# The 7x7 convolution of a two-block kernel: banded weight rows loaded to half of the partitions, and copied by VectorE to the other half

## The chip, the cores and the metric

The kernel runs on one core of one Trainium2 chip. Its metric is the device time of one execution in microseconds (us). Three runs of the kernel before took 6082.45, 6082.88 and 6088.8 us; the median is 6082.88.

The engines have short names in the profile: PE is TensorE (matrix products), PEld its weight loads, DVE is VectorE, ACT is ScalarE, POOL is GpSimd and SP is SyncE. SP, ScalarE and GpSimd can issue DMAs; GpSimd's have the DMA queue q0, and SP's have q1.

## The reference

The input x has 8 images of 96 x 96 pixels with 192 channels in fp32. The first block normalises x by groups, projects it to 384 channels, applies a depthwise 3x3 convolution and four running averages, normalises over channels, projects back and adds x. The second block is the one that matters here:

```python
def _L1_conv_ref(x, dw_kernel, dw_bias, ln_gamma, ln_beta, w0, b0, w1, b1, gamma):
    y = lax.conv_general_dilated(x, dw_kernel, window_strides=(1, 1), padding='SAME',
            dimension_numbers=('NHWC', 'HWIO', 'NHWC'), feature_group_count=c) + dw_bias
    ...
    y = (y - mu) * lax.rsqrt(var + EPS) * ln_gamma + ln_beta
    y = jnp.einsum('bhwc,cd->bhwd', y, w0) + b0
    y = jax.nn.gelu(y, approximate=False)
    y = jnp.einsum('bhwd,dc->bhwc', y, w1) + b1
    return y * gamma

x = x + _L1_conv_ref(_gn(x), ...)
```

`_gn` is the normalisation over 32 groups of 6 channels of each image. The convolution is depthwise: each channel has its own 7 x 7 filter (the weights are `dw_kernel`, 7 x 7 x 1 x 192).

## The kernel before

The work runs in five stages, each with its own pools of tiles, and each ends before the next one's products begin: the first projection (to about 847 us of the span), the 3x3 convolution with the running averages (to 1885), the second projection of the first block (to 3003), the 7x7 convolution (to 3590) and the two dense layers of the second block (to the end). In each stage the order of instructions on every engine is the order of the program (`tc.manual_schedule()`); nothing is reordered by a planner.

**The 7x7 convolution as products.** Its input lies in DRAM as `X1_d`, by rows and by three column phases; 21 image rows times 3 phases make 63 lines, which lie on 63 of 64 partitions. A product of TensorE contracts over these 63 lines with a band matrix, which holds the filter's taps along a diagonal band, so that one product gives the outputs of 63 lines for one horizontal offset. The bands of all channels were prepared in DRAM as `Z2_d` (64 rows, 192 channels, `ZW` = 208 numbers). The stage uses the two halves of the partitions at the same time: the lower half (0 to 63) works on row blocks 0, 2 and 4, the upper half (64 to 127) on row blocks 1, 3 and 5. Both halves contract with the same band, and since a product reads its weights from the partitions that its data are on, the band has to be in both halves.

**Loads.** The 192 channels make 32 groups m of `HC` = 6 channels. `load_d(m)` loads what one group needs: a tile `xin`, in three pieces t for each half (384 KB each, line 748), and a tile `band`, one load for each half (64 partitions of 6 x 208 numbers, 4992 bytes each, 312 KB, line 753). What goes to the lower half is issued by SP, what goes to the upper half by GpSimd. So each of the two queues carries three pieces of xin and one band for each group. Five groups can be held at a time (`ND` = 5: one buffer that is there early, and four more in the pool `d_in`); a load waits for its buffer's last reader on TensorE.

**Scaling.** `scale_d(m, xin)` applies the group normalisation to xin in place, with one VectorE instruction for each of the 8 images (line 1006).

**Products and stores.** `conv_d` makes the products of one channel for a pair of groups (line 1021), which ScalarE brings from PSUM into the tile `yo` with the bias (line 1032). `store_d` writes `yo` to DRAM as `Y_d`, with 16 DMAs from GpSimd a turn (line 1061); the last turn divides them between SP and GpSimd (line 1060). A turn of the loop handles a pair of groups, and there are 16 turns. Turn i first issues the loads of groups 2i+3 and 2i+4, then the scaling of groups 2i+2 and 2i+3 for the next turn, then the products of groups 2i and 2i+1, and then its stores:

```python
for i in range(n_i):
    pair, loads = loads[:2], loads[2:]
    for m in (2 * i + 3, 2 * i + 4):
        if m < 2 * n_i:
            loads.append(load_d(m))
    if i + 1 < n_i:
        for k in range(2):
            scale_d(2 * i + 2 + k, loads[k][1])
```

On GpSimd's queue a turn is therefore eight loads, which are the three pieces and the band of the odd group and then those of the even group, and after them sixteen stores. A DMA of this queue waits until the DMA eight places ahead of it has landed, because eight semaphores are used in turn. SP's queue has the same eight loads, and no stores except in the last turn. VectorE has only the scalings in this stage.

The functions that the change touches, with the lines of the profile:

Of the kernel before, what the change touches and what calls it, by code (L numbers as in the profile page):

```python
# [84 lines left out]
def conv_blocks_kernel(  # L85
# [31 lines left out]
    nc = tc.nc  # L117
# [44 lines left out]
    Z2_d = dram.tile([64, D, ZW], F32, name="Z2_d")  # L162
# [126 lines left out]
    with ExitStack() as ph:  # L289
# [175 lines left out]
        with tc.manual_schedule():  # L465
# [9 lines left out]
            for b in range(B):  # L475
                more = b + 1 < B
                for t in range(n_t):
# [27 lines left out]
                    k, j = divmod(t, NJ)  # L505
# [32 lines left out]
    with ExitStack() as ph:  # L538
# [13 lines left out]
        def load_b(k):  # L552
            c = slice(k * CC, (k + 1) * CC)
            band = bp_.tile([128, CC, 3, RB], F32, tag="band", name=f"band0_{k}")
            pin = bp_.tile([128, CC, GB, NJ, S], F32, tag="pin", name=f"pin_{k}")
            for g in range(NG):
                p = g * 64
                nc.sync.dma_start(
                    band[p : p + RB + 4].rearrange("p c t o -> p (c t o)"),
                    ZB_d[:, c].rearrange("r c t o -> r (c t o)"),  # L560
                )
                for lo, hi in ((0, RB), (RB, RB + 1), (RB + 1, RB + 2)):
                    nc.sync.dma_start(
                        pin[p + lo : p + hi].rearrange("p c b j h -> p c (b j h)"),
                        P_d[g, c, lo:hi].rearrange("c r b j h -> r c (b j h)"),
                    )
            return band, pin
# [71 lines left out]
        with tc.manual_schedule():  # L639
            loads = [load_b(k) for k in range(3)]  # L640
# [8 lines left out]
            for n in range(NI * (n_k + 1)):  # L649
                k, i = divmod(n, NI)  # L650
                z = None
                if k < n_k:
                    if i == 0:
                        band, pin = loads.pop(0)
# [48 lines left out]
    def make_weights(ps):  # L703
        for m in range(NE):
            for p, k, _ in spans[:2]:
                nc.tensor.matmul(
                    ps[:, m : m + 1],
                    w0w[p, k, m * 128 : (m + 1) * 128],
                    aff[p, k, 1:2],
                    start=(k == 0),  # L710
                    stop=(k == 1),
                )
        nc.vector.tensor_tensor(b1g, b1g, lsc, ALU.mult)
        for m in range(NE):
            nc.vector.tensor_tensor(w1g[:, m], w1g[:, m], lsc, ALU.mult)
        nc.vector.tensor_tensor(b0g, b0g, ps[:, :NE], ALU.add)
        for k in range(3):
            nc.vector.tensor_scalar(w0w[:, k], w0w[:, k], aff[:, k, 0:1], None, ALU.mult)
# [9 lines left out]
    HC = GS  # L728
# [6 lines left out]
    def load_d(m):  # L735
        c = m * HC
        row = D * WV * 2
        pool = d_pools[m % ND > 0]
        xin = pool.tile([128, NT, BP, HC, 2 * WV], F32, tag="xin", name="xin")

        for t in range(NT):
            for g, eng in enumerate((nc.sync, nc.gpsimd)):
                src = bass.AP(
                    tensor=X1_d.tensor,
                    offset=X1_d.offset + (2 * t + g) * HG * PH * row + c * WV * 2,
                    ap=[[row, 64], [S * PH * row, BP], [1, HC * WV * 2]],
                )
                eng.dma_start(
                    xin[g * 64 : (g + 1) * 64, t].rearrange("q a c n -> q a (c n)"), src
                )  # L750
        band = pool.tile([128, HC, ZW], F32, tag="band", name="band1")
        for g, eng in enumerate((nc.sync, nc.gpsimd)):
            eng.dma_start(
                band[g * 64 : (g + 1) * 64].rearrange("q c l -> q (c l)"),
                Z2_d[:, c : c + HC].rearrange("r c l -> r (c l)"),
            )
        return band, xin

    s1 = s1_pool.enter_context(tc.tile_pool(name="s1", bufs=1)).tile(
# [2 lines left out]
    with ExitStack() as ph:  # L762
# [175 lines left out]
        with tc.manual_schedule():  # L938
            load_weights()
            for u in range(n_u + 1):  # L940
# [22 lines left out]
                if held is not None:  # L963
                    k, t = divmod(u - 1, n_c)
# [8 lines left out]

            stores.pop(0)()
            first_d = load_d(0)
            for store in stores:
                store()
# [10 lines left out]
    with ExitStack() as ph:  # L988
# [9 lines left out]
                dw_bias.rearrange("(i k c) -> k i c", k=2, c=HC)[k].partition_broadcast(64),  # L998
            )

        def scale_d(m, xin):
            xv = xin.rearrange("q t a c (v b) -> q t a c v b", b=2)
            for b in range(B):
                sc, sh = (s1[:, a, b % 2, b // 2, m : m + 1] for a in range(2))
                xw = xv[:, :, b // 2, :, :, b % 2]
                nc.vector.tensor_scalar(xw, xw, sc, sh, ALU.mult, ALU.add)  # L1006
# [33 lines left out]
        def store_d(yo, i):  # L1040
            for bl in range(NB):

                pieces = [(3, HB - 3)]
                if bl == 0:
                    pieces.append((HB - 3, HB))
                if bl == NB - 1:
                    pieces.append((0, 3))
                for k in range(2):
                    c = i * CD + k * HC
                    for lo, hi in pieces:  # L1050
                        r = (S - HB - bl * HG) * PH
                        src = yo[k * 64 + lo * PH : k * 64 + hi * PH, bl]
                        dst = Y_d[r + lo * PH : r + hi * PH, :, :, c : c + HC].rearrange(
                            "r b a c n -> r (b a) (c n)"
                        )
                        src = src.rearrange("r a c n -> r a (c n)")

                        n = NV if i == D // CD - 1 else 0
                        if n:
                            nc.sync.dma_start(dst[:, :n], src[:, :n])  # L1060
                        nc.gpsimd.dma_start(dst[:, n:], src[:, n:])

        n_i = D // CD
        with tc.manual_schedule():
            loads = [first_d] + [load_d(m) for m in range(1, 3)]
            make_weights(ps_y.tile([128, 512], F32, tag="py1", name="ps_b0"))
            for m in range(2):
                scale_d(m, loads[m][1])
            for i in range(n_i):
                pair, loads = loads[:2], loads[2:]  # L1070
                for m in (2 * i + 3, 2 * i + 4):
                    if m < 2 * n_i:
                        loads.append(load_d(m))
                if i + 1 < n_i:
                    for k in range(2):
                        scale_d(2 * i + 2 + k, loads[k][1])
                yo = op.tile([128, NB, BP * NV, HC, 2 * WQ], F32, tag="yo", name=f"yo_{i}")
                for c in range(HC):
                    conv_d(pair, c, yo, i)
                store_d(yo, i)  # L1080
# [233 lines left out]
```

## Time and profile before

| What | Value |
|---|---|
| median of 3 runs | 6082.88 us |
| the profiled execution's own time | 6083.09 us |
| its span, from the first to the last instruction | 6081.0 us |
| 7x7 stage, 3003 to 3590 us | 587 us |
| PE busy in that stage | 414.21 us |
| DVE busy in that stage | 167.40 us |
| POOL busy in that stage | 245.80 us |
| products of line 1021 | 6912 |
| scalings of line 1006 | 256, median 665 ns |
| loads of band, line 753 | 32 from SP and 32 from GpSimd |
| HBM read, written | 585.19 MB, 476.57 MB |

The profile comes from one execution. It records for every instruction its engine, line, operation, start and duration, and what ended the idle time before it. A line of a view in order of time begins with the start and the duration in us; "x432" says that so many instructions are merged into it, and "[7.95 <-DVE xin L1006]" that the engine had been idle for 7.95 us until VectorE's instruction of line 1006, which writes xin, had ended. In rows of 40 slices, each digit is the busy share of a slice in tenths. "DMA share" is the mean busy share of the 16 DMA engines, and PEclk the granted clock of TensorE as a share of full speed. A DMA that GpSimd issues shows as a POOL instruction, whose duration is that of the issue; the transfer itself comes later.

### The profile page before, as it was taken

What the parts mean: (1) busy time and instruction counts of PE and PEld (TensorE: products, weight loads), DVE (VectorE), ACT (ScalarE), POOL (GpSimd) and SP (SyncE); (2) the same over time, 40 slices, a digit from 0 to 9 for tenths busy, and PEclk for the clock granted to TensorE, in tenths of its full rate; (3) what the DMA queues carried; (4) which work ended last, traced back from release to release, by engine and by line L of the source; (5) the groups of instructions that cost most, each with busy time, mean ns of one, the idle gap of its engine ahead of it and who ended that gap; (6) DMA issues with size and microseconds to landing.
All of it is one profiled execution on the core that took longest, in us unless ns stands there. A gap on an engine that the chain in (4) does not pass through costs nothing.

```text
span 6081.0 us, 122820 instructions
## 1 busy us (share of the span) xinstructions
PE 5685.5 (93%) x48550; PEld 3948.3 (65%) x48550; DVE 3456.3 (57%) x8026; ACT 2438.4 (40%) x6146; POOL 2632.8 (43%) x2832
## 2 busy tenths in 40 slices
PE   4899989999998999999777759999999999999999
PEld 2455543333335989898666647777777777777777
DVE  5455539999996667777632334444444444444442
ACT  2344447777775555555433322222222222222221
POOL 0111128888886666666544433222222222322222
PEclk9899989999999999999888879999999999999999
DMA  8987669999997888888799962222222222222221
GB/s 238 230 246 238 210 191 244 245 245 242 244 244 203 253 261 267 262 265 263 230 287 286 291 167 78 63 78 62 78 62 77 63 78 63 78 63 78 63 63 37
DMA packets 570206, 1054.36 MB, mean 173 GB/s; under 512 B 109575, under 2 KB 426260, under 8 KB 567328
## 3 DMA queue, kind: packets, MB, share of 16 engines
q1 hardware_dynamic: 385312, 577.65, 35.9%
q0 software_dynamic: 124160, 450.67, 23.9%
q10 hardware_dynamic: 60160, 18.20, 1.5%
q8 instruction: 384, 6.29, 0.5%
q14 instruction: 190, 1.56, 0.1%
HBM read 585.19 MB, written 476.57 MB: 175 GB/s over the span
## 4 chain that ended last, share of the span: by engine, by line
PE 75%; DMA 7%; DVE 1%; issue 1%; POOL 1%; SPq 1%; ACT 0%; POOLq 0%; DVEq 0%; ACTq 0%
PE po L1213 19%; PE po L830 13%; PE hp L1183 12%; PE pl L576 10%; PE hp L1193 7%; PE pa L597 4%; PE pt L828 4%; DMA xin<-X_d 4%; PE pt L1166 2%; PE pa L600 2%; DMA Y_d<-yo 2%; PE py L1021 1%; DMA band<-Z_d 1%; DVE xin L1006 0%; SPq L1060 0%
## 5 line engine op out<-in xcount | busy, mean ns | idle before, releaser
L1202 ACT ACTIVATE g<-hp,b0g 128x384 f32<-128x384 f32 x1152 | 573.9, 580 | 1856.3 <-PE hp L1193 1856.3
L1213 PE MATMUL po<-w1g,g 128*128 128x192 f32 x6912 | 1178.3, 327 | 0.0
L1213 PEld LDWEIGHTS po<-w1g,g 128*128 128x128 f32 x6912 | 1116.6, 190 | 1.6 <-issue 1.1
L830 PE MATMUL po<-wc,mt 128*96 128x193 f32 x4608 | 913.3, 334 | 0.0
L1170 DVE COPY yT<-pt 128x384 f32<-128x384 f32 x288 | 251.4, 873 | 1126.9 <-PE pt L1166 1126.6
L1231 POOL DMA_DIRECT2D out_dram<-xo x576 | 321.2, 560 | 1148.0 <-DVE xo L1220 1119.5
L1183 PE MATMUL hp<-yT,w0w 128*128 128x384 f32 x2304 | 794.5, 488 | 0.4 <-ACT g L1202 0.4
L830 PEld LDWEIGHTS po<-wc,mt 128*96 128x96 f32 x4608 | 702.3, 163 | 68.4 <-ACT mean L834 65.0
L576 PE MATMUL pl<-pin,band 34*32 34x380 f32 (+1 forms) x13824 | 628.6, 489 | 18.5 <-DMA pin<-P_d 18.5
L1183 PEld LDWEIGHTS hp<-yT,w0w 128*128 128x128 f32 x2304 | 431.5, 191 | 231.5 <-issue 2.8
L606 DVE TENSOR_TENSOR_SCAN z<-decay,loc 128x768 f32<-128x768 f32 x288 | 505.8, 1756 | 59.1 <-ACT loc L585 29.3
L1021 PE MATMUL py<-xin,band 63*64 63x248 f32 (+1 forms) x6912 | 405.9, 393 | 141.6 <-DVE xin L1006 139.6
L646 POOL TENSOR_TENSOR mo<-mo,z 128x768 f32<-128x768 f32 x288 | 529.4, 1839 | 3.4 <-ACT mo L601 0.4
L615 DVE TENSOR_TENSOR_SCAN z<-decay,z 128x768 f32<-128x768 f32 x288 | 498.1, 1730 | 0.0
L576 PEld LDWEIGHTS pl<-pin,band 34*32 34x32 f32 x13824 | 233.1, 107 | 396.1 <-issue 394.8
L1021 PEld LDWEIGHTS py<-xin,band 63*64 63x64 f32 x6912 | 343.4, 142 | 203.7 <-DVE xin L1006 125.6
L837 ACT ACTIVATE sq<-pt,mean 96x384 f32<-96x384 f32 x768 | 442.9, 577 | 25.9 <-ACT mean L834 1.0
L1193 PE MATMUL hp<-yT,w0w 64*128 64x384 f32 x2304 | 449.5, 508 | 0.0
L597 PE MATMUL pa<-loc,mix 128*32 128x384 f32 x3456 | 431.9, 493 | 0.0
L600 PE MATMUL pa<-last,down 96*32 96x384 f32 x1152 | 426.8, 493 | 0.9 <-ACT mo L601 0.9
L29 POOL TENSOR_TENSOR rs<-rs_ve,neg_half 96x8 f32<-96x8 f32 x96 | 158.6, 1652 | 607.1 <-DVE rs_ve L28 607.1
L375 PE MATMUL pm<-xT,win 128*128 128x384 f32 x1152 | 401.5, 500 | 20.0 <-ACT xT L368 19.7
(116 smaller groups left out, 7712.8 us busy)
## 6 DMA issues: line engine op xcount, KB each, us to landing
P_d<-po POOLq DMA_DIRECT2D x96, 1152.0 KB, 8.8
pin<-P_d SPq DMA_DIRECT2D x192, 576.0 KB
mt<-M_d SPq DMA_DIRECT2D x576, 192.0 KB
xq<-in_x_dram SPq DMA_DIRECT2D x96, 576.0 KB
xr<-in_x_dram SPq DMA_DIRECT2D x384, 144.0 KB
X_d<-x1u POOLq DMA_DIRECT2D x192, 288.0 KB, 4.1
X_d<-x1c SPq DMA_DIRECT2D x192, 288.0 KB
y<-Y_d SPq DMA_DIRECT2D x24, 2304.0 KB
```

The source lines that it names most:

```text
L576: nc.tensor.matmul(pls[g][at * RB : (at + 1) * RB, :, lo:hi], band[rows, c, kh, :], pin[rows, c, :, NJ - 1 - j, lo + kh - 1 : hi + kh - 1] ...
L597: nc.tensor.matmul(pa[at], mix[:, i, at], loc[:, q], start=True, stop=True)
L600: nc.tensor.matmul(pa[at], down[:, to], last[:, q], start=True, stop=True)
L606: nc.vector.tensor_tensor_scan(zf, decay_f, loc.rearrange("p q n -> p (q n)"), 0.0, ALU.mult, ALU.add)
L615: nc.vector.tensor_tensor_scan(zr, decay_f, zr, 0.0, ALU.mult, ALU.add)
L646: nc.gpsimd.tensor_tensor(m, m, z, ALU.add)
L830: nc.tensor.matmul(po[:S, b], lhs[m], wc[:, m], start=(m == 0), stop=(m == NC - 1))
L1021: nc.tensor.matmul(pys[t // 2][g][k * 64 : (k + 1) * 64, t % 2, :, lo:hi], pair[k][0][rows, c, d * ZS : d * ZS + 64], pair[k][1][rows, t, ...
L1183: nc.tensor.matmul(hps[m, q], w0w[:, 2 * q, m * 128 : (m + 1) * 128], yT[:, 2 * q], start=True, stop=False,)
L1193: nc.tensor.matmul(hps[m, q], w0w[p, 1, m * 128 : (m + 1) * 128], yT[p, 1], start=False, stop=True,)
L1202: nc.scalar.activation(g[:, m, q], hps[m, q], AF.Gelu, bias=b0g[:, m : m + 1], scale=1.0)
L1213: nc.tensor.matmul(po[:, q], g[:, m, q, k * 128 : (k + 1) * 128], w1g[:, m], start=(m == 0), stop=(m == NE - 1),)
```

## The change

`load_d` issues one load of the band in place of two. For an even group it is SP's, into the lower half of the partitions, and for an odd group GpSimd's, into the upper half. `scale_d` is given the band as well, and begins with a VectorE copy of the loaded half to the other one, ahead of the eight scalings of the group.

```diff
         band = pool.tile([128, HC, ZW], F32, tag="band", name="band1")
-        for g, eng in enumerate((nc.sync, nc.gpsimd)):
-            eng.dma_start(
-                band[g * 64 : (g + 1) * 64].rearrange("q c l -> q (c l)"),
-                Z2_d[:, c : c + HC].rearrange("r c l -> r (c l)"),
-            )
+
+        g = m % 2
+        (nc.sync, nc.gpsimd)[g].dma_start(
+            band[g * 64 : (g + 1) * 64].rearrange("q c l -> q (c l)"),
+            Z2_d[:, c : c + HC].rearrange("r c l -> r (c l)"),
+        )
         return band, xin
...
-        def scale_d(m, xin):
+        def scale_d(m, band, xin):
+            g = m % 2
+            nc.vector.tensor_copy(
+                band[(1 - g) * 64 : (2 - g) * 64], band[g * 64 : (g + 1) * 64]
+            )
             xv = xin.rearrange("q t a c (v b) -> q t a c v b", b=2)
             for b in range(B):
...
             for m in range(2):
-                scale_d(m, loads[m][1])
+                scale_d(m, *loads[m])
...
                     for k in range(2):
-                        scale_d(2 * i + 2 + k, loads[k][1])
+                        scale_d(2 * i + 2 + k, *loads[k])
```

The products of line 1021 wait for VectorE's copy where they waited for a DMA of the band; their number, order and operands stay as they were.

## The prediction

> **What bounds the kernel now.** I read the page first, then the busy time by stage, then the 7x7 stage alone: PE and VectorE in order of time, the DMA traffic of two of its turns, and GpSimd's queue in order of time. The page:
>
> ```profile
> span 6081.0 us, 122820 instructions
> PE   4899989999998999999777759999999999999999
> DMA  8987669999997888888799962222222222222221
> ```
>
> Only the dip of PE near slice 20 is touched. The profiled execution took 6083.09 us, 2.1 us more than its span; the median of the runs shown is 6082.88, so its own sum can stand for it. Busy time of each engine in the 7x7 stage and in the one behind it:
>
> ```profile
> core 0: us, PE busy (x) PEld busy (x) DVE busy (x) ACT busy (x) POOL busy (x), PEclk, DMA share, GB/s
> 3003.00:3590.00 587.00, 414.21 (x6944) 350.95 (x6944) 167.40 (x303) 201.50 (x384) 245.80 (x385) 0.83 0.99 269
> 3590.00:6081.00 2491.00, 2449.93 (x12672) 1828.41 (x12672) 1124.06 (x2976) 575.22 (x1153) 729.10 (x768) 0.99 0.25 69
> ```
>
> In its 587 us PE works 414 and the DMA engines all the time. Three of the sixteen turns on PE, and the scalings of xin on DVE around them (start, duration, and in brackets the idle time before and what ended it):
>
> ```profile
> 3214.14 25.68 PE L1021 MATMUL py<-xin,band 63*64 63x256 f32 x432 [7.95 <-DVE xin L1006]
> 3248.66 25.49 PE L1021 MATMUL py<-xin,band 63*64 63x256 f32 x432 [8.84 <-DVE xin L1006]
> 3280.78 25.28 PE L1021 MATMUL py<-xin,band 63*64 63x256 f32 x432 [6.63 <-DVE xin L1006]
> ```
> ```profile
> 3243.87 4.74 DVE L1006 TENSOR_SCALAR xin<-xin,s 128x576 f32<-128x576 f32 x8 [20.99 <-DMA xin<-X_d]
> 3250.69 4.80 DVE L1006 TENSOR_SCALAR xin<-xin,s 128x576 f32<-128x576 f32 x8 [2.09 <-DMA xin<-X_d]
> 3275.98 4.74 DVE L1006 TENSOR_SCALAR xin<-xin,s 128x576 f32<-128x576 f32 x8 [20.49 <-DMA xin<-X_d]
> ```
>
> PE idles 7 to 9 us a turn, for DVE, which has itself been idle 20 us for xin. From the turn that starts at 3082.15 to the last at 3546.67 there are 14 periods: 33.18 us each. The scaling at 3243.87 is that of the odd group (m = 2i+3), which PE needs at once; that at 3250.69 is the even one for the turn after. Traffic from 3214 to 3282, in 40 slots of 1.7 us:
>
> ```profile
> GB/s 305 373 328 340 297 342 325 384 393 394 386 328 202 209 206 200 204 205 195 289 340 362 316 308 348 398 382 388 369 342 305 231 212 200 209 208 199 201 235 301
> q0 software_dynamic: 4128, 13.57, 73.2%
> q1 hardware_dynamic: 3780, 6.29, 30.7%
> ```
>
> q0 is GpSimd's queue, q1 SP's (packets, MB, share of the 16 engines' time). SP moves less than half as much and spends its time waiting for PE to free a buffer (258.5 us for xin, line 748, between 3083 and 3572). So GpSimd's queue is the long one: 8 loads and 16 stores a turn. How it runs:
>
> ```profile
> 3237.12 0.54 POOL L753 DMA_DIRECT2D band<-Z_d x1 [0.52 <-DMA Y_d<-yo]
> 3239.51 0.70 POOL L1061 DMA_DIRECT2D Y_d<-yo x1 [1.85 <-ACT yo L1032]
> 3240.52 0.58 POOL L1061 DMA_DIRECT2D Y_d<-yo x1 [0.30 <-DMA xin<-X_d]
> 3243.76 0.80 POOL L1061 DMA_DIRECT2D Y_d<-yo x1 [2.66 <-DMA xin<-X_d]
> 3245.07 0.56 POOL L1061 DMA_DIRECT2D Y_d<-yo x1 [0.51 <-DMA band<-Z_d]
> 3247.32 0.73 POOL L1061 DMA_DIRECT2D Y_d<-yo x1 [1.68 <-DMA xin<-X_d]
> 3248.83 0.63 POOL L1061 DMA_DIRECT2D Y_d<-yo x1 [0.78 <-DMA xin<-X_d]
> 3250.59 0.81 POOL L1061 DMA_DIRECT2D Y_d<-yo x1 [1.13 <-DMA xin<-X_d]
> 3252.03 0.62 POOL L1061 DMA_DIRECT2D Y_d<-yo x1 [0.64 <-DMA band<-Z_d]
> ```
>
> Each store waits for the DMA eight places ahead to land, so these starts are the landings of the loads, one behind another without a gap: xin third piece at 3243.76, band at 3245.07, then the even group's pieces and its band at 3252.03. The stores are issued while up to 12 us of loads are still ahead of them. A period is this queue's work: by the landings about 16 us of loads and 17 of stores. The flat slots near 203 GB/s are its loads alone.
>
> **The change part by part.** Each group's band is now one load of 64 x 4992 bytes = 0.32 MB in place of two: even groups on SP into the lower half, odd ones on GpSimd into the upper. A turn fetches one odd and one even group, so each queue loses one band of two a turn.
>
> (1) GpSimd's queue, on the path. A band there cost 1.31 us (3243.76 to 3245.07) and 1.44 (3250.59 to 3252.03); its bytes at 203 GB/s are 1.57. I take 1.45; ends 1.3 and 1.6. The even bands of m = 4 to 30 fall in the 14 periods.
>
> (2) SP's queue, beside it. That band only shares the 16 DMA engines with GpSimd's stores. From below it is 0: between 3572 and 3610, after all loads of the stage, its last stores and the next stage's first load move 201 GB/s, so stores don't take up all that is left to them. From above: both bands at the mean rate of these two turns (294 GB/s) are 0.64/0.294 = 2.17 us, less 1.45 leaves 0.7. I take 0.3, nearer to the row of stores alone. The queue alone would then need 33.18 - 1.45 - 0.3 = 31.4.
>
> (3) The copies, 32 of 64 x 1248 on DVE. Bounds by element: the contiguous scaling of w0w (line 718, 768 in 615 ns) gives 1.00 us, the strided copy of x1c (line 866, 768 in 1050 ns) 1.71. I take 1.0, since operands here are contiguous too. The even one has cover: its group lands a turn ahead; if that cover went, it would cost 1.0 a turn. The odd one has none.
>
> (4) A new wait. scale_d now starts with the copy, and the copy waits for the band, behind the three xin pieces on its queue. Queued behind it on DVE are the eight scalings of the same group and the next group's copy and scalings; PE waits for those, ScalarE for PE, GpSimd's stores for ScalarE. Before, the band landed during the scaling. So the odd group's scaling starts 1.45 + 1.0 = 2.45 us later against its xin (ends 1.3 + 1.0 and 1.6 + 1.71).
>
> (5) What that delay meets. It lies on a loop of two periods: odd xin landed, scaling, PE turn, first store issued (3243.87 to 3273.84: 30.0 us), then 16 stores and three xin pieces until the next odd scaling (3239.51 to 3275.98: 36.5). Sum 66.5, two periods. Part of it is queueing: the store issued at 3239.51 had loads ahead until 3252.03 (12.5 us), that of 3273.84 until about 3283.9, where a store starts again (10). A DMA of this stage with little ahead took 5.9 us to land (fastest xin, line 748). So 10 - 5.9 = 4.1 to 12.5 - 5.9 = 6.6 of the loop is slack: without it 59.9 to 62.4. With the 2.45: 62.4 to 64.9, or 31.2 to 32.4 a period. Queue (31.4) and loop (31.2 to 32.4) now lie together. I take 31.8, their middle: 1.38 saved x 14 = 19.3 us.
>
> (6) Ends. The second turn starts at 3082.15 when SP's last xin of group 3 has landed; one SP band ahead of it goes (0.32 MB at 203 GB/s, 1.6) and a copy of 1.0 comes: -0.6. The last turn has no ring behind it: its scaling waits for band and copy, +2.4. Sum +1.8.
>
> 6083.1 - 19.3 + 1.8 = 6065.6; I say 6065. Nothing else moves: PE's, ScalarE's and the stores' instructions stay in their order, and the last stage's PE (2450 of 2491 us) is the same work.
>
> A rule speaks against (3). The Trainium skill, page "SBUF — State Buffer", section "SBUF: two separate sides", says that a VectorE copy of fp32 within SBUF locks GpSimd out of a shared port, so that it can't write the descriptors of its DMAs; the page has such a DMA go from about 620 to 3100 ns. In this trace, GpSimd's issues that begin beside a scaling took 0.56 to 0.81 us, others 0.54 to 0.70, and it idles 72.6 us between 3114 and 3517 for landed xin alone: by the rows nothing. By the rule, an estimate: 28 copies x 2.5 us = 70 if each hit an issue on the path, ending at about 6135.
>
> **The rivals.**
>
> DMA time alone counts, and the loop has more slack than I give it. Both bands go in full, 2.17 a period, 30 in all, and with the -0.6 and +2.4 it ends at 6054; by the ends of (2) and a start gain of some us, down to 6045. For it: DMA share 0.99 in the whole stage. Against: SP is idle for PE part of each turn.
>
> The gain is given back. The period stays at 32.4 to 33.2 because the loop is at its upper end, or copies take 1.71: 0 to 11 us less, +1.8: 6074 to 6085. For it: PE waits for DVE every turn. Against: stores with 10 us of loads ahead of them. Here belongs also that the transfers were hidden anyway.
>
> Slower: the band lands late. It is the last of its group, and one load must now feed both halves. If it landed only with the even group's xin (three pieces, some 2 us apart, 5.9 us later), the loop would be 62.4 + 2.45 + 5.9 = 70.8, 35.4 a period: +2.2 x 14 + 1.8 = +33, 6116. It decides once the loop gains more than 66.4 - 62.4 = 4.0 us, a band 3.0 us behind its xin. Against: 1.31 us in the rows above.
>
> **How the numbers follow.** 0.2% is 12 us, about what a measurement of this kernel can tell from no change. Forecast (6056 to 6071): 0.42. DMA time alone (below 6056): 0.21. Given back (6071 to 6095): 0.24. Slower: 0.13. So faster 0.63, same 0.24, slower 0.13. The range, 6045 to 6095, leaves out the late band and a little below. The forecast's own range is 6056 to 6071.
>
> **What will show it.** Right: 16 bands on each queue; 32 copies near 1.0 us, the odd ones after a wait for band; PE's turns 31.8 us apart with 6.5 idle; HBM read 10.2 MB less than 585.19; other stages unchanged. (1) fails if GpSimd's loads still take 16 us a turn; (4) and (5) if PE starts no later after the odd xin, or if the stores find the queue drained. It is wrong if the copy takes over 2 us, if GpSimd's issues stretch beside it, or if the band lands well behind its xin.

## The result and the profile after

The changed kernel took 6091.97 us in the median (6082.58 to 6095.32), the kernel before 6082.66 in the same comparison (6079.82 to 6088.8). The ratio after to before is 1.0011, with a 95% interval of 0.9994 to 1.0029: no difference that can be measured. 6065 us were forecast. What came about is the case that the prediction calls "the gain is given back".

The profiled execution took 6094.07 us. The rows of its page that answer those of before (its span, PE's and the DMA engines' busy tenths, the HBM traffic):

```profile
span 6091.8 us, 122792 instructions
PE   4899989999998999999768769999999999999999
DMA  8987769999997888888799962222222222222221
HBM read 574.97 MB, written 476.57 MB: 173 GB/s over the span
```

The reads fell from 585.19 to 574.97 MB, which is 10.22 MB, or 32 loads of 64 x 4992 bytes: the bytes are gone. The span is 10.8 us longer than before's, but not because of the stage that was changed. That stage, from the last product of the third stage to the first product of the fifth with its dense weights (line 1183 before, 1188 after), takes 624.8 us before and 623.9 after (worked out from the starts and ends of those products). The third stage ends 10.2 us later (3002.4 against 2992.2), in work that the change does not touch and that varies from one execution to the next: in another execution of the changed kernel it ends at 2992.8. The last stage is 1.5 us longer. So the account is -0.9 + 10.2 + 1.5 = 10.8, and what is to be explained is why the 7x7 stage kept its length.

Busy time in the 7x7 stage, with the window of before set 10.2 us later, where the stage now lies:

```profile
core 0: us, PE busy (x) PEld busy (x) DVE busy (x) ACT busy (x) POOL busy (x), PEclk, DMA share, GB/s
3013.20:3600.20 587.00, 417.13 (x6944) 342.80 (x6944) 194.46 (x335) 201.59 (x384) 236.73 (x369) 0.84 0.96 252
```

PE and ScalarE do the work of before (414.21 and 201.50 us there); VectorE has 27 us more, of which its 32 copies are 25.8 (32 x 0.805). The mean rate is 252 GB/s where it was 269. PE's turns in order of time, three that were not broken:

```profile
3194.24 24.72 PE L1026 MATMUL py<-xin,band 63*64 63x256 f32 x432 [8.20 <-DVE xin L1011]
3361.50 24.71 PE L1026 MATMUL py<-xin,band 63*64 63x256 f32 x432 [8.63 <-DVE xin L1011]
3392.07 24.79 PE L1026 MATMUL py<-xin,band 63*64 63x256 f32 x432 [5.85 <-DVE xin L1011]
```

PE still waits 6 to 9 us a turn for VectorE. Below, a "period" is the mean distance of PE's turns from the turn with index 2 (the third) to the last, thirteen of them, by their starts in this view. A turn's start is that of the products that need its odd group; the four records ahead of them need the even group alone and can run before. The prediction's 33.18 was taken over fourteen distances, from the turn before. Before, the period is (3546.67 - 3113.69)/13 = 33.31 us, after (3556.37 - 3128.13)/13 = 32.94. Over the prediction's fourteen it is 33.18 before and (3556.37 - 3089.67)/14 = 33.34 after, where 31.8 was forecast. VectorE in order of time:

```profile
3220.18 1.03 DVE L1004 COPY band<-band 64x1248 f32<-64x1248 f32 x1 [20.36 <-DMA band<-Z_d]
3221.24 4.74 DVE L1011 TENSOR_SCALAR xin<-xin,s 128x576 f32<-128x576 f32 x8
3226.02 0.80 DVE L1004 COPY band<-band 64x1248 f32<-64x1248 f32 x1
3226.85 4.88 DVE L1011 TENSOR_SCALAR xin<-xin,s 128x576 f32<-128x576 f32 x8
```

The odd group's copy waits for the landing of the band, and its scaling, which PE needs, comes behind it; the even copy has cover. So steps (3) and (4) are there as predicted. GpSimd's queue in order of time, the first stores of three turns:

```profile
3218.65 3.36 POOL L1066 DMA_DIRECT2D Y_d<-yo  x5 [8.81 <-ACT yo L1037]
3251.60 3.98 POOL L1066 DMA_DIRECT2D Y_d<-yo  x6 [7.63 <-ACT yo L1037]
3287.97 3.97 POOL L1066 DMA_DIRECT2D Y_d<-yo  x6 [9.80 <-ACT yo L1037]
```

In the rows of before, the first store of the turn waited 1.85 us for ScalarE, and each of the next ones for a landing. Now the first of a turn waits 8 to 10 us for ScalarE's output in these rows, and 3 to 10 in the others. The longest waits of GpSimd's stores between 3114 and 3517 (total, times, longest), first of before, then of after:

```profile
POOL Y_d L1061 <- DMA xin<-X_d: 72.6, 53, 3.0
POOL Y_d L1061 <- ACT yo L1032: 40.1, 16, 4.7
```
```profile
POOL Y_d L1066 <- ACT yo L1037: 80.7, 13, 10.1
POOL Y_d L1066 <- DMA xin<-X_d: 29.5, 31, 2.7
```

The wait for landed xin fell by 43 us, and the wait for ScalarE rose by 41. The queue got shorter, and GpSimd spends what it gained on waiting for the products, which come no earlier. The DMA traffic of the same window (packets, bytes, mean rate; then, for the stores, issues, size and the median us from issue to landing), of before and of after:

```profile
DMA packets 45725, 115.91 MB, mean 288 GB/s; under 512 B 7428, under 2 KB 27714, under 8 KB 45673
Y_d<-yo POOLq DMA_DIRECT2D x144, 270.0 KB, 8.8
```
```profile
DMA packets 43811, 108.88 MB, mean 270 GB/s; under 512 B 7066, under 2 KB 27120, under 8 KB 43762
Y_d<-yo POOLq DMA_DIRECT2D x144, 270.0 KB, 8.8
```

There are 6% fewer bytes at a rate 6% lower, in the same time. And the median of the large stores is 8.8 us with the shorter queue as with the longer one; by their place in the turn they differ, as step (5) below shows.

### The profile page after: what moved, and what is told of

It is laid out like the page before. It is cut to its first block, busy times and chain, and to the rows that moved or that the text cites. A ratio compares the mean times of both kernels' runs of the same rounds, so it can differ in the third digit from the quotient of the medians.

```text
span 6091.8 us, 122792 instructions
## 1 busy us (share of the span) xinstructions
PE 5697.4 (94%) x48550; PEld 3942.0 (65%) x48550; DVE 3484.5 (57%) x8058; ACT 2438.8 (40%) x6146; POOL 2623.2 (43%) x2816
## 3 DMA queue, kind: packets, MB, share of 16 engines
HBM read 574.97 MB, written 476.57 MB: 173 GB/s over the span
## 4 chain that ended last, share of the span: by engine, by line
PE 77%; DMA 6%; DVE 1%; SPq 1%; issue 1%; POOL 0%; ACT 0%; POOLq 0%; ACTq 0%; DVEq 0%
PE po L1218 19%; PE po L831 13%; PE hp L1188 12%; PE pl L576 10%; PE hp L1198 7%; PE pa L597 4%; PE pt L829 4%; PE py L1026 3%; DMA xin<-X_d 3%; PE pt L1171 2%; PE pa L600 2%; DMA Y_d<-yo 2%; DVE xin L1011 1%; DMA band<-Z_d 0%; SPq L1065 0%
```

## The experiments

The theory with which they began: the stage follows the loop of step (5), two periods long, which has less slack than was taken, so that the 2.3 us by which the odd scaling starts later cost the whole gain. The rivals: the copies slow GpSimd or the memory down where they run; the missing traffic was hidden anyway; the loss lies at the start. All ratios are to the kernel before, run on the same chip, with their 95% intervals. The period, and the length of the 7x7 stage as defined above, come from one profiled execution of each kernel. Edits are shown against the changed kernel, if nothing else is said.

| Kernel | ratio to before | period, us | stage, us |
|---|---|---|---|
| before | 1 | 33.31 | 624.8 |
| after | 1.0011 [0.9994, 1.0029] | 32.94 | 623.9 |
| repeat (after once more) | 1.0007 [0.9998, 1.0016] | 33.05 | 627.1 |
| no_copy | 0.9972 [0.9962, 0.9982] | 31.79 | 607.5 |
| copy_last | 0.9992 [0.9984, 1.0001] | 32.14 | 615.0 |
| copies4 | 1.0046 [1.0033, 1.0059] | 35.23 | 661.4 |
| copy_only | 1.0019 [1.0010, 1.0029] | 33.73 | 635.0 |
| even_only | 0.9980 [0.9972, 0.9989] | 31.82 | 607.8 |
| odd_only | 1.0003 [0.9994, 1.0012] | 32.58 | 622.3 |
| sp_both | 0.9994 [0.9985, 1.0003] | 31.81 | 610.3 |
| band_first | 0.9992 [0.9983, 1.0002] | 32.86 | 623.9 |
| act_copy | 0.9971 [0.9962, 0.9980] | 31.76 | 607.0 |
| even_stores | 1.0047 [1.0036, 1.0059] | 35.51 | 657.5 |
| before_stores | 1.0070 [1.0058, 1.0082] | 36.19 | 667.0 |

The last of the thirteen distances is shorter in most kernels (25 to 33 us). Without it, before stands at 33.6, the changed kernel at 33.0 and 33.3, and the four kernels that gain most a period (no_copy, even_only, sp_both, act_copy) at 32.0 to 32.4. So the order stays, and a period is known to some 0.3 us.

**The same kernel once more.** No edit.

> The changed kernel once more. Mark to read: the mean distance of PE's turns from the third (i = 2) to the last, 33.31 us before and 32.94 after, and the products' turn itself, 25.1 to 26.9 us before and 24.7 to 29.9 after. Loop theory (the copy and its wait lengthen a loop of two periods by 2.3 us and eat what the queue saves): 32.9 again, the same total as before within 0.2%. Fetch theory (the loss lies in pauses inside PE's turns, 'issue', which after the change came in 8 of 13 turns, 0.3 to 2.6 us each): pauses in most turns again; if they were chance, few pauses and a period near 32.

It took 1.0007 [0.9998, 1.0016], with a period of 33.05 us. The two executions agree within 0.11 us a period. The longer span of the first was its early stages. PE's turns had pauses in 3 of 13, and the period did not come near 32, so the pauses do not carry the loss.

**The loads without the copy.** The products of the half that is not loaded take a constant tile as weights, so no copy is needed, and their output is not the convolution.

```diff
         def scale_d(m, band, xin):
-            g = m % 2
-            nc.vector.tensor_copy(
-                band[(1 - g) * 64 : (2 - g) * 64], band[g * 64 : (g + 1) * 64]
-            )
...
-                                pair[k][0][rows, c, d * ZS : d * ZS + 64],
+                                pair[k][0][rows, c, d * ZS : d * ZS + 64]
+                                if g == k
+                                else neg_half[rows],
```

> The changed kernel's loads without the copy: for the half whose band is not loaded, the products take a constant tile as weights, so those outputs are not the convolution. The traffic is the changed kernel's, the order on DVE that of before. Loop theory: queue 31.4 and loop 30 to 31.2, so a period of 31.4 to 31.8 and 20 to 25 us less than before in all (about 6060). Rival (the bands' transfers were hidden anyway): 33.3 and no difference from before. Fetch theory: the period stays at 32.5 or more because of pauses in PE's turns.

The period fell to 31.79 us, and the kernel is faster by 0.28%, some 17 us; the stage is 17.3 us shorter. A row of VectorE in order of time:

```profile
3253.21 4.74 DVE L1007 TENSOR_SCALAR xin<-xin,s 128x576 f32<-128x576 f32 x8 [20.09 <-DMA xin<-X_d]
```

The odd scaling starts again when xin has landed. So the missing traffic is worth at least 1.5 us a period, and the rival that it was hidden anyway falls. What takes this back comes with the copies.

**The copy behind the scalings.**

```diff
         def scale_d(m, band, xin):
-            g = m % 2
-            nc.vector.tensor_copy(
-                band[(1 - g) * 64 : (2 - g) * 64], band[g * 64 : (g + 1) * 64]
-            )
             xv = xin.rearrange("q t a c (v b) -> q t a c v b", b=2)
...
                 nc.vector.tensor_scalar(xw, xw, sc, sh, ALU.mult, ALU.add)
+            g = m % 2
+            nc.vector.tensor_copy(
+                band[(1 - g) * 64 : (2 - g) * 64], band[g * 64 : (g + 1) * 64]
+            )
```

> The changed kernel with the copy behind the eight scalings of its group instead of ahead of them; all bytes and queues as in the changed kernel. Loop theory: scaling starts when xin has landed, only the copy's 0.8 us stays between xin and PE in place of 2.3, so a loop of two periods is 1.5 us shorter, the period 32.2 in place of 32.9, 10 us less than the changed kernel in all. Rival (the transfers never counted, the period is set elsewhere): 32.9, no difference. Fetch theory alone: 32.9, with the pauses still there.

The period is 32.14 us and the ratio 0.9992 [0.9984, 1.0001]. VectorE in order of time:

```profile
3252.70 4.75 DVE L1007 TENSOR_SCALAR xin<-xin,s 128x576 f32<-128x576 f32 x8 [18.03 <-DMA xin<-X_d]
3257.47 0.80 DVE L1009 COPY band<-band 64x1248 f32<-64x1248 f32 x1
```

The band lands during the scaling, and only the copy's own 0.80 us is left between xin and PE. All copies are made, by the same engine, and two thirds of the gain in the period are back: (32.94 - 32.14)/(32.94 - 31.79) = 0.7. In time that is not enough to be measured.

**The odd copy four times.**

```diff
-            nc.vector.tensor_copy(
-                band[(1 - g) * 64 : (2 - g) * 64], band[g * 64 : (g + 1) * 64]
-            )
+            for _ in range(4 if g else 1):
+                nc.vector.tensor_copy(
+                    band[(1 - g) * 64 : (2 - g) * 64], band[g * 64 : (g + 1) * 64]
+                )
```

> The changed kernel with the copy of each odd group made four times over, 2.4 us more ahead of its scalings; nothing else moves. Loop theory: half of the delay goes into the period, 33.0 + 1.2 = 34.2, 16 us more than the changed kernel (about 6107). If slack takes it up: 33.0, the changed kernel's time.

The period rose to 35.23 us, 1 us more than the loop theory had, and the time by 0.46%. VectorE in order of time:

```profile
3228.74 3.45 DVE L1005 COPY band<-band 64x1248 f32<-64x1248 f32 x4 [21.57 <-DMA band<-Z_d]
3232.21 4.75 DVE L1012 TENSOR_SCALAR xin<-xin,s 128x576 f32<-128x576 f32 x8
```

With these the loop can be read. Let d be the delay: the mean time from the landing of the odd group's last piece of xin to PE's turn, over the turns with index 2 to 13, less that of `no_copy`, from the single records.

| Kernel | d, us | two periods, us | more than no_copy |
|---|---|---|---|
| no_copy | 0 | 63.6 | |
| copy_last | 0.9 | 64.3 | 0.7 |
| after, repeat | 2.3, 2.1 | 65.9, 66.1 | 2.3, 2.5 |
| copies4 | 4.7 | 70.5 | 6.9 |

Up to 2.3 us, two periods grow by about d: the mark of a loop of two periods with no slack left, as step (5) drew it. In copies4 they grow by 2.2 us more than d. There PE's turn itself is longer: 1.9 us more than in `no_copy` pass from its start to the first store, and pauses in the midst of the turns, for which the profile shows no wait, add up to 1.5 us a turn. They lie on the same loop. So copies4 is no clean reading of the delay alone; why PE pauses more there was not tried.

**The copy alone, with both halves loaded as before.** The edit is against the kernel before; the copy writes the loaded half onto itself.

```diff
-        def scale_d(m, xin):
+        def scale_d(m, band, xin):
+            g = m % 2
+            nc.vector.tensor_copy(band[g * 64 : (g + 1) * 64], band[g * 64 : (g + 1) * 64])
```

> Both halves of every band loaded as in the kernel before, and on top of it a copy per group in the changed kernel's place, of a loaded half onto itself: it waits for the same band and costs the same 0.8 us, and nothing is saved. The runs so far give the periods 31.8 (no copy), 32.1 (copy behind the scalings, 0.8 us late) and 33.0 (copy ahead, 2.3 late), that is half of each delay. If the loop of two periods also sets the period of the kernel before (33.31): 33.3 + 2.3/2 = 34.4, 15 us more than before. If there the queue sets it with the 4 us of slack in the loop that the prediction read from the trace: 33.3 to 33.5, no difference.

1.0019 [1.0010, 1.0029], some 12 us, with a period of 33.73 us. The odd group waits here too for band and copy, 2.5 us more than before by the records. Two periods grow by 2 x (33.73 - 33.31) = 0.84. So some 2.5 - 0.84 = 1.7 us found slack in the loop of the kernel before; the price lies between "no slack" and "hidden".

**One parity alone.** `even_only` makes the change for even groups only, `odd_only` for odd ones only; the other groups keep both loads and no copy. The edit of `even_only` (`odd_only` has `m % 2 == 1 and g != 1`, and `if g == 1`):

```diff
-        g = m % 2
-        (nc.sync, nc.gpsimd)[g].dma_start(
-            band[g * 64 : (g + 1) * 64].rearrange("q c l -> q (c l)"),
-            Z2_d[:, c : c + HC].rearrange("r c l -> r (c l)"),
-        )
+        for g, eng in enumerate((nc.sync, nc.gpsimd)):
+            if m % 2 == 0 and g != 0:
+                continue
+            eng.dma_start(
+                band[g * 64 : (g + 1) * 64].rearrange("q c l -> q (c l)"),
+                Z2_d[:, c : c + HC].rearrange("r c l -> r (c l)"),
+            )
...
-            nc.vector.tensor_copy(
-                band[(1 - g) * 64 : (2 - g) * 64], band[g * 64 : (g + 1) * 64]
-            )
+            if g == 0:
+                nc.vector.tensor_copy(
+                    band[(1 - g) * 64 : (2 - g) * 64], band[g * 64 : (g + 1) * 64]
+                )
```

> The change for even groups alone: their band is loaded by SP and copied, the odd groups load both halves as before and have no copy. GpSimd's queue loses the same band as in the changed kernel, SP's loses none, and no copy stands between an odd xin and PE. Loop theory: 31.8 to 32.1, 16 to 20 us less than before (about 6067). If SP's missing band was what gained in the run without copies: 33.0 to 33.3.

> The change for odd groups alone: their band is loaded by GpSimd and copied, even groups load both halves. GpSimd's queue carries what it carried before, SP's loses one band a turn, and the copy and its wait (2.3 us) stand between an odd xin and PE. Loop theory: the delay without the gain, 33.3 to 34.4, 0 to 15 us more than before. If the copy's place is harmless and bytes count: 33.0, a few us less than before.

The even half is faster by 0.20%, 1.0 - 0.9980, with a period of 31.82 us: half of the loads removed, no delay for the odd group, and as much gained a period as without any copy. The odd half has a ratio of 1.0003 and a period of 32.58: the other half of the loads removed, and nothing gained in time. Its period lies below all that was expected of it (33.0 to 34.4): with an odd delay added and GpSimd's queue as long as before, it is 0.7 us shorter, so the band that SP no longer loads seems to count too. Both together are the changed kernel, with nothing gained either. So the even band's saving, which is worth 33.31 - 31.82 = 1.5 us a period by itself, is worth nothing once the odd delay is there (32.58 without it, 32.94 and 33.05 with it). Such parts do not add up; the longer of two bounds, queue or loop, decides, as step (5) had it. VectorE of `even_only`:

```profile
3244.41 4.74 DVE L1014 TENSOR_SCALAR xin<-xin,s 128x576 f32<-128x576 f32 x8 [19.23 <-DMA xin<-X_d]
3249.18 0.80 DVE L1007 COPY band<-band 64x1248 f32<-64x1248 f32 x1
```

The odd scaling follows xin, and the even copy comes while PE already has what it needs.

**All bands by SP.** Every band is loaded to the lower half by SP and copied to the upper one; GpSimd carries no band.

```diff
-        g = m % 2
-        (nc.sync, nc.gpsimd)[g].dma_start(
-            band[g * 64 : (g + 1) * 64].rearrange("q c l -> q (c l)"),
+        nc.sync.dma_start(
+            band[:64].rearrange("q c l -> q (c l)"),
             Z2_d[:, c : c + HC].rearrange("r c l -> r (c l)"),
         )
...
-            nc.vector.tensor_copy(
-                band[(1 - g) * 64 : (2 - g) * 64], band[g * 64 : (g + 1) * 64]
-            )
+            nc.vector.tensor_copy(band[64:], band[:64])
```

> The changed kernel with every band loaded by SP into the lower half and copied to the upper one. SP's queue runs ahead of GpSimd's, so the copy's band has landed long before xin. Loop theory: the copy runs while DVE waits for xin and costs nothing; GpSimd's queue loses both bands of a turn, 2.9 us, and needs 30.4; the loop needs 30 to 31.2; period 31, 30 us less than before (about 6053). Rival (SP's queue becomes the late one, since it starts behind PE's end and shares the engines): odd scalings wait for SP's xin, period 32.5 to 33.5. Rival (transfers hidden): 33.3.

The period is 31.81 us. VectorE in order of time:

```profile
3234.04 0.80 DVE L1002 COPY band<-band 64x1248 f32<-64x1248 f32 x1 [7.15 <-DMA band<-Z_d]
3250.57 4.82 DVE L1007 TENSOR_SCALAR xin<-xin,s 128x576 f32<-128x576 f32 x8 [15.73 <-DMA xin<-X_d]
```

The odd copy is done 16 us ahead of the scaling, so there is no delay. But GpSimd's queue is shorter by another band than in `even_only`, and the period is the same. Four kernels with no delay and different loads on that queue (`no_copy`, `even_only`, `sp_both`, and `act_copy` below) stand at 31.76 to 31.82. For `even_only` alone the queue, 33.31 - 1.45 = 31.9, would say the same. For `sp_both`, whose queue lacks two bands, it would not: 31.8 fits the loop's own length, 63.5 to 63.6 for two periods. In time `sp_both` missed what it was given: 0.9994 [0.9985, 1.0003], though its stage is 14.5 us shorter in the profiled execution. Its start is the slowest of the kernels without delay (the turn with index 2 starts 127.9 us after the third stage's last product, against 121.5 before). That accounts for a stage gain of 14.5 in place of 13 x 1.5 = 19.5, but not for a gain of only some 4 us in the ratio; this stays open.

**The band ahead of xin.** In `load_d` the load of the band comes before the three pieces of xin.

```diff
         xin = pool.tile([128, NT, BP, HC, 2 * WV], F32, tag="xin", name="xin")
+        band = pool.tile([128, HC, ZW], F32, tag="band", name="band1")
+
+        g = m % 2
+        (nc.sync, nc.gpsimd)[g].dma_start(
+            band[g * 64 : (g + 1) * 64].rearrange("q c l -> q (c l)"),
+            Z2_d[:, c : c + HC].rearrange("r c l -> r (c l)"),
+        )
...
-        band = pool.tile([128, HC, ZW], F32, tag="band", name="band1")
-
-        g = m % 2
-        (nc.sync, nc.gpsimd)[g].dma_start(
-            band[g * 64 : (g + 1) * 64].rearrange("q c l -> q (c l)"),
-            Z2_d[:, c : c + HC].rearrange("r c l -> r (c l)"),
-        )
         return band, xin
```

> The changed kernel with each group's band loaded ahead of its three xin pieces on the queue in place of behind them. The copy can then run while DVE waits for xin, but xin lands a band's transfer (1.45 us) later. Loop theory: a delay of 1.45 in place of 2.3, period about 32.5 against 33.0, 6 us less than the changed kernel (about 6085). If it is the copy's 0.8 us alone that hurts: 31.8, as without copies.

The copy now runs early, but xin lands behind the band, so 1.45 us of the delay stay. The period is 32.86 us, the stage 623.9, the time 0.9992 [0.9983, 1.0002]. By the loop, two periods would be 63.6 + 1.45 = 65.0; they are 65.7. By the records each piece of xin is also issued later, since the band takes the place ahead of it in the queue: the first one 1.7 us after the landing of the ninth store, where the other kernels take 0.6. The place of the wait changes little: what the band's transfer takes on the odd group's way to PE counts, ahead of xin or behind it.

**The copies on ScalarE.** They are made at the end of a turn, behind its last bias operation, for the two groups of the next turn. The edit against the changed kernel:

```diff
-        def scale_d(m, band, xin):
+        def copy_d(m, band):
             g = m % 2
-            nc.vector.tensor_copy(
-                band[(1 - g) * 64 : (2 - g) * 64], band[g * 64 : (g + 1) * 64]
-            )
+            nc.scalar.copy(band[(1 - g) * 64 : (2 - g) * 64], band[g * 64 : (g + 1) * 64])
+
+        def scale_d(m, xin):
...
             for m in range(2):
-                scale_d(m, *loads[m])
+                copy_d(m, loads[m][0])
+                scale_d(m, loads[m][1])
...
-                        scale_d(2 * i + 2 + k, *loads[k])
+                        scale_d(2 * i + 2 + k, loads[k][1])
...
+                if i + 1 < n_i:
+                    for k in range(2):
+                        copy_d(2 * i + 2 + k, loads[k][0])
                 store_d(yo, i)
```

> The changed kernel with the copies made by ScalarE, for the next turn's two groups behind a turn's last evacuation of products, in place of VectorE ahead of the scalings. All loads are the changed kernel's. Loop theory: the odd band lands 1.45 us behind its xin and a ScalarE copy of some 1.3 us runs beside the 4.75 us of scalings, so nothing is added between xin and PE: 31.8 a period as without copies, 17 to 20 us less than before (about 6069). If any reader of the late band hurts, or ScalarE's wait holds up the evacuation of the next turn: 33 or more and the changed kernel's time.

0.9971 [0.9962, 0.9980], a median of 6071.56 us against 6091.94 for the kernel before on that chip, and a period of 31.76 us. It beats both kernels. ScalarE, VectorE and PE in order of time:

```profile
3243.71 1.23 ACT L1004 COPY band<-band 64x1248 f32<-64x1248 f32 x1
3245.88 1.23 ACT L1004 COPY band<-band 64x1248 f32<-64x1248 f32 x1 [0.94 <-DMA band<-Z_d]
```
```profile
3244.68 4.74 DVE L1011 TENSOR_SCALAR xin<-xin,s 128x576 f32<-128x576 f32 x8 [20.22 <-DMA xin<-X_d]
```
```profile
3249.52 24.94 PE L1026 MATMUL py<-xin,band 63*64 63x256 f32 x430 [3.89 <-issue]
```

The odd copy waits for the band and ends at 3247.11, while VectorE scales that group's xin until 3249.42; PE's turn begins 0.10 us after that. The same copies, half as long again (1.23 us against 0.80), cost nothing that shows in this place, where the odd one stands beside the scaling and not in front of it.

**Four of the sixteen stores by SP.** This was to take load from GpSimd's queue, with the change for even groups (`even_stores`) and in the kernel before (`before_stores`). The edit, the same in both:

```diff
-                        nc.gpsimd.dma_start(dst[:, n:], src[:, n:])
+                        eng = nc.sync if not n and bl in (2, 3) else nc.gpsimd
+                        eng.dma_start(dst[:, n:], src[:, n:])
```

> The kernel with the change for even groups alone, and 4 of the 16 stores of a turn (row blocks 2 and 3) issued by SP in place of GpSimd, except in the last turn. Loop theory: the loop of two periods runs through GpSimd's 16 stores at 1.05 us each; 4 fewer make it 4.2 us shorter, 2.1 a period: 29.7 against 31.8, 27 us less than with the even groups alone (about 6047). If the 16 DMA engines are the limit, whichever queue feeds them: 31.8 and no gain.

> The kernel before with the same 4 stores of a turn issued by SP, and both halves of every band loaded. Loop and queue theory: GpSimd's queue, 33.3 us of work a turn, loses 4.2: 29 to 31.2 a period, 27 to 50 us less than before. If the 16 DMA engines are the limit: 33.3 and no gain.

Both came out slower, by 0.47% and 0.70%, with periods of 35.51 and 36.19 us: the loop theory had the wrong sign. The DMA traffic of `before_stores` between 3114 and 3517:

```profile
DMA packets 54431, 105.36 MB, mean 261 GB/s; under 512 B 6547, under 2 KB 40635, under 8 KB 54384
```

Compared with the kernel before, there are 9% fewer bytes in that window, in 19% more packets: those under 2 KB rose from 27714 to 40635, those of 2 KB and more fell from 18011 to 13796. By the single records, GpSimd's stores go out as packets of 4608 bytes, and the same stores issued by SP as packets of 768. The edit also put the stores ahead of SP's loads in its queue: in that window SP's wait for PE to free a buffer fell from 241.8 us to 64.4, and GpSimd's stores waited 149.0 us for ScalarE where they had waited 40.1, so SP's queue was no longer the one with time to spare. The edit thus changed the kind of transfer and the late queue together, and the two runs say nothing for or against the loop. What the even groups' missing bands are worth shows here as well: 36.19 - 35.51 = 0.7 us a period.

## Why the prediction was right or wrong

The time came out inside the stated range: 6091.97 us, against 6045 to 6095. It is 27 us above the forecast of 6065 and outside the forecast's own range, 6056 to 6071. What came about had the chance 0.24, not the 0.42 of the forecast. That the range held, by 3 us, is owed to its width, which took in the rivals, and to luck; the sum itself failed in step (5).

**Step (1) held, step (2) was too small.** Each queue issues 16 bands. GpSimd's block of loads, by the landings, takes 14.8 us a turn in place of 16.4 (means of ten turns). `even_only`, where GpSimd's queue alone loses a band, gains 1.5 us a period; (1) had 1.45. `odd_only`, where SP's alone loses one, gains 0.7 with an odd delay on top, so SP's band seems worth at least that (one execution of each); (2) took 0.3, and 0.7 as its upper end. This is no matter for the result, since the queue is not what decides after the change.

**Step (3) was a little too dear.** The copy's median is 805 ns (803 to 1031), predicted was 1.0. The rule that was weighed there (the Trainium skill, "SBUF — State Buffer", section "SBUF: two separate sides"), by which such a copy would have locked GpSimd out of writing descriptors, does not show in a cost. GpSimd's issues of Y_d took 557 / 648 / 963 ns (least, median, most) before and 557 / 651 / 1210 after, 256 of each; 35 of those after ran beside a copy, with a median of 676. `sp_both`, whose VectorE makes all 32 copies, has the period of `no_copy`, which makes none (31.81 and 31.79 us). The estimate of 70 us by the rule finds nothing to stand on in this case.

**Step (4) held.** The odd group's scaling starts later for the band (about 1.5 us) and the copy (0.8): 2.3 and 2.1 us in the two executions, where 2.45 were predicted.

**Step (5) is where it failed: the slack of the loop.** The loop itself was right, two periods long, and the path through it too. The prediction held 4.1 to 6.6 us of its 66.5 for queueing that would go away, all of it between a turn's first store and the landing of xin, so that the 2.45 us of delay would fit into it. The loop's parts, from the issue, landing and start of the single records (rounded means in us of the turns with index 2 to 13):

| Part | before | after | repeat | no_copy |
|---|---|---|---|---|
| odd xin landed, to PE's turn | 5.2 | 7.5 | 7.3 | 5.2 |
| PE's turn, to its first store's issue | 25.1 | 25.6 | 25.0 | 24.8 |
| first store's issue, to the landing of the odd xin behind the stores | 36.5 | 33.2 | 34.2 | 33.9 |
| sum | 66.7 | 66.3 | 66.5 | 63.9 |
| in the third part: landing of the first store | 13.4 | 8.6 | 9.1 | 10.4 |
| in the third part: landing of the ninth store | 7.8 | 9.6 | 10.0 | 8.3 |

The third part was to shrink from 36.5 to between 29.9 and 32.4; it shrank to 33.2 and 34.2. So the slack was 2.3 to 3.3 us, about as much as the delay took, and not 4.1 to 6.6. (`copy_only` uses 1.5 of it, and `odd_only`, at 33.5, shows 3.0.) The term that was mis-sized is the landing. Step (5) subtracted 5.9 us, the fastest xin of the stage, as what a DMA with little ahead of it takes. The first store of a turn does land much sooner with the shorter queue, but in 8.6 and 9.1 us, not 5.9. And the ninth store, which waits for it and for which the first xin piece waits in turn, takes about 2 us longer than before. The median over all large stores, 8.8 us in both kernels, hides these two changes. That it is SP's loads which the stores meet then is an argument only.

"Queue (31.4) and loop (31.2 to 32.4) now lie together" thus became a loop alone, at 32.94 to 33.05, 0.26 to 0.37 below the 33.31 of before. Over 13 periods that is 3.4 to 4.7 us, where 19.3 were predicted over 14.

**Step (6) was wrong too, by about 5 us.** It gave the start a gain of 0.6 us. By the products' starts, against the end of the third stage, the turn with index 1 begins 87.3 us later in place of 89.9 before, a gain of 2.6; but the next one begins after 125.7 in place of 121.5, a loss of 4.2. The DMA rate from 3030 to 3130 (slots of 2.5 us), of after:

```profile
GB/s 311 311 307 300 199 22 264 233 251 279 280 289 272 281 284 282 295 272 230 197 202 202 161 75 166 227 262 355 361 362 305 316 269 206 202 203 278 318 327 341
```

From 3085 to 3092.5 it falls to 161, 75 and 166 GB/s; the row of before has no such hole at this place of its stage. All loads that have a buffer are done, the others wait for the first turn's products to free one, and the first stores leave 85.7 us after the third stage in place of 85.0. The start's gain is spent waiting. `no_copy`, which has no delay, begins the turn with index 2 after 124.6, so most of the loss comes without the copies; the odd delay, which (6) charged only to the last turn, can be no more than the rest. From there 0.37 x 13 of the loop and 0.4 at the end make the 0.9 us by which the stage is shorter: 4.2 - 4.7 - 0.4 = -0.9.

**The rivals.** "The gain is given back" named the reason that held: the loop at its upper end. The argument against it, "stores with 10 us of loads ahead of them", took the same slack as (5). "DMA time alone counts" fails with `copy_last` and `act_copy`: they move the bytes of the changed kernel, and their periods are 0.8 and 1.2 us shorter. "The band lands late" did not happen: it lands about 1.5 us behind xin, as read from before. With the slack as measured, it would have decided from 2.3 to 3.3 us on, and not from 4.0.

## What to carry to other kernels

When a stage is bound by a queue, look at once for the loop that stands just behind it, and count what is in it: a shorter queue is worth only the distance to that loop, and an operation put into the loop without slack is paid nearly in full. For the slack in a loop, do not subtract the fastest transfer of the stage: here the first store took 8.6 to 9.1 us with its queue drained, where 5.9 were taken, and a later one grew by 2. Follow the transfers of the loop by their place in the turn; a median over all of them showed no change. And where a copy is put mattered more here than its engine or its length: 1.23 us on ScalarE beside the scaling cost nothing that shows, 0.80 us in front of the consumer, with the wait that it brought along, cost the whole gain.

## What was not expected of the hardware

**PE pauses in the midst of a turn.** In the profiled execution of the changed kernel 6 of the turns with index 2 to 14 are broken, by nine pauses of 0.3 to 2.6 us, for which the profile shows no wait. PE in order of time:

```profile
3258.35 7.09 PE L1026 MATMUL py<-xin,band 63*64 63x256 f32 x96 [4.15 <-DVE xin L1011]
3268.07 15.44 PE L1026 MATMUL py<-xin,band 63*64 63x256 f32 x256 [2.63 <-issue]
```

Each ends 1.3 to 1.8 us after a packet of 16384 bytes has landed on queue q8, which the profile calls "instruction"; the one that started at 3265.7 took 0.96 us, and PE goes on at 3268.07. Such packets come about as often in the kernel before (41 against 40 between 3114 and 3517), which had one small pause. It looks as if PE waited for its instructions behind the other traffic. No run tests this. It is not what took the gain: the second execution of the changed kernel had three pauses, in 3 of 13 turns, and a period within 0.11 us.

**The packets of a store changed with the engine that issued it.** As told above, they have 768 bytes from SP and 4608 from GpSimd, and the window moved 261 GB/s in place of 288. Moving four of sixteen stores cost 2.9 us a period in the kernel before; how much of that is the packets and how much SP's longer queue was not tried.

**GpSimd's queue alone moves some 200 GB/s.** Its loads go to one half of the partitions. The flat slots of 197 to 206 in the row above are such stretches, while slots in which both queues move reach 300 to 362. Whether the one half is the reason was not tried. Between the turns with index 2 and 15, the time in which SP moves nearly nothing (under 15 GB/s) grew from 9.0 us a period to 10.4, and 11.2 in the second execution (slots of 0.5 us). The lower mean rate goes with that. It does not decide the time, since `act_copy` has 11.2 too, and is faster.
